# Bias reads at the end of step 4 over two DMA queues, eight products for the first four slots, and the first image's combinations spread over slots 0 to 3

## The chip, the core and the metric

The kernel runs on one core of a Trainium2 chip. A core has five engines that run their own instruction streams: TensorE (PE in the profile, with its weight loads as PEld), VectorE (DVE), ScalarE (ACT), GpSimd (POOL) and SyncE (SP). SP computes nothing here; it issues nearly all DMAs. ACT issues a few DMAs too, between its own operations. An instruction that waits holds up everything behind it on the same engine, and that is true of a DMA-issuing instruction on SP or ACT as well. The metric is the device time of one execution in microseconds (us); lower is better.

## The reference, cut to what matters

The input x has 4 images of 32 by 32 positions with 768 channels. Two layers follow each other. Each one normalizes x over 32 channel groups, runs attention with 12 heads of 64 channels over the 1024 positions of an image, and adds the result to x:

```
x = x + attention0(group_norm(x))
x = x + attention1(group_norm(x))
# attention: q, k, v = x @ W (+ bias in layer 1)
#   scores = scale * q k^T + rel_h[query, key_row] + rel_w[query, key_col]
#   out = softmax(scores) @ v, then @ Wproj + bproj
```

The bias of the scores depends on the query itself: rel_h and rel_w are products of q with a table of 63 relative positions per axis, of which each query uses a different stretch of 32. Everything is float32.

## The kernel before, in words

**Slots and steps.** The 2 layers times 4 images give 8 images in sequence, each with 6 pairs of heads. The 48 pairs are called slots here (`g` in the code, 0 to 47). A slot has 8 steps (`n`), one for each block of 128 queries, so there are 384 steps. All instructions are written out in one fixed order (`tc.manual_schedule`); nothing reorders them later. In the listing, `units` is the list of steps, and the loop over it is the body of the kernel.

**What a step does.** It is a pipeline three steps deep:

- `biases` for the step after next: two POOL additions (L461) spread the two bias axes over 128 x 1024 tiles `sc`, one for each head.
- `scores` for the next step: PE multiplies q and k (L475), DVE combines products and bias and finds the maximum (L484), ACT takes the exponential and its sum (L488).
- `turn` for this step: DVE transposes the finished `sc` into a buffer `tb` (L518). Every second step SP writes `tb` to DRAM as `td` (L521, 1 MB for each head). This covers two steps, a quarter of the slot.
- `divide` for the next step: DVE takes the reciprocal (L495); POOL scales one head (L502), ACT the other (L504).

**Reading back and weighing.** The four quarters of `td` are read back in another order as `pt` (L531, 1 MB for each head), through the lists `behind` and `behind2`: quarter 0 is read at step 3, quarter 1 at step 4, quarter 2 at step 7, and quarter 3 at step 0 of the next slot. A read waits for the write to have landed. At the end of step 6 PE multiplies quarters 0 and 1 with v (L550, `weigh`), and at the end of step 2 of the next slot quarters 2 and 3.

**Work for other slots.** During slot g, PE also runs the projections of slot g+1 (`prepare`), the values of a pair of slots and a share of the output projection of this or the previous image (`put_out`, L629). `shares[n]` says how many pieces of it a step takes after its scores.

**Eight products or seven.** `project_in` has two forms, and `plain(g)` chooses. The plain form multiplies the two halves of q's and k's weights with the two halves of the image: four units of 6 pieces. The other form needs 3.5 units (6, 3, 6 and 6 pieces) but works on sums and differences that have to be made first. Those of the weights are made by `sum_weights` (one ACT copy L330 at the end of step 6 two slots ahead, three POOL operations L333 to L335 at the end of step 7), by a DVE copy (L274) in the middle of unit 0 and a POOL subtraction (L301) after it. Those of the image are made by `sum_input`: it fills spare tiles y and z and changes the image's own tiles in place. In numbers, for an image: 6 ACT copies (L348) and 6 POOL subtractions for y, 6 POOL additions (L351) and 3 ACT copies (L353) for z, then 6 and 6 POOL subtractions in place, all 24 POOL operations on 64 x 512. Before, the plain form is used for the first slot of each image and slot 1:

```
    def plain(g):
        return g % NP == 0 or g == 1
```

For all images but the first, `sum_input` runs in slots 4 and 5 of the image before and in its own slot 0. For the first image it runs in slot 0 (18 POOL operations) and slot 1 (6).

**The bias tables.** `positions(g, i)` multiplies q with the tables on PE (L408), copies the result on ACT (L418), and writes one axis to DRAM as `tdr` from ACT's queue (L420). The other axis is cut out by 32 small ACT copies (L431), which wait in the list `last`, and a step's end takes 8 or 16 of them. `diagonals(g)` reads the first axis back along diagonals into `rel1`: 8 DMAs of 32 KB, 4 for each head (L447). Before, it goes through the list `later`, so that it is issued at the start of step 4 of the slot before. All 8 are on SP, except for slot 0. The POOL addition of step 6 is the first that reads `rel1` for the next slot.

**The order on SP.** In step 4, SP's stream holds: any loads of the next image's x (L117, in the fifth slot of an image), the 8 diagonal reads, a weight load (L131), the first two residual tiles for `put_out` (L608, `fetch`), the read-back of quarter 1; in step 5, two more residual tiles and the write of quarter 2. `fetch` has its place in the step ahead of the read-backs. Its tiles share 4 buffers with the tables' copies.

Of the kernel before, what the change touches and what calls it, by code (L numbers as in the profile page):

```python
# [48 lines left out]
NC = C // P  # L52
# [6 lines left out]
NP = NH // 2  # L59
# [7 lines left out]
def attention_blocks(ctx: ExitStack, tc: tile.TileContext, a: dict, out: bass.AP):  # L67
    nc = tc.nc
# [22 lines left out]
    mid = [dram.tile([C, S], FP, tag=f"mid{b}", name=f"mid{b}") for b in range(B)]  # L91
# [4 lines left out]
    NPAIR = NI * NP  # L96
# [138 lines left out]
    qk_of, v_of, rel_of, t_of = {}, {}, {}, {}  # L235

    def plain(g):
        return g % NP == 0 or g == 1

    def add(to, t, x, bias=None):  # L240

# [94 lines left out]

        return first, second

    def sum_input(im, n):

        xs, ys = x_of[im], y_of[im]

        def each(chunks):
            return [(c, xs[c], xs[NC + c], ys[c], ys[NC + c % 3], TOP if c < 3 else LOW) for c in chunks]

        sub = lambda out, x, y: nc.gpsimd.tensor_tensor(out, x, y, ALU.subtract)  # L346
        for c, a, b, y, z, half in each({-1: (0, 1, 2), 0: (3,), 1: (4,), 2: (5,)}.get(n, ())):
            nc.scalar.copy(y[LOW], b[TOP])  # L348
            sub(y[TOP], b[LOW], y[LOW])
        for c, a, b, y, z, half in each({1: (0,), 2: (1, 2), 3: (3,), 4: (4, 5)}.get(n, ())):  # L350
            nc.gpsimd.tensor_tensor(z[half], y[TOP], a[TOP], ALU.add)  # L351
            if half == TOP:
                nc.scalar.copy(y[LOW], z[TOP])  # L353
        for c, a, b, y, z, half in each({5: (0,), 6: (1, 2), 7: (3, 4, 5)}.get(n, ())):
            sub(b[TOP], b[TOP], a[TOP])
        for c, a, b, y, z, half in each({9: (0, 1, 2), 10: (3, 4, 5)}.get(n, ())):
            sub(y[LOW], (y if half == TOP else z)[LOW], a[LOW])

    def project_values(g, i):

        im, pair = divmod(g, NP)
        xs, w = x_of[im], w_of[g, 2]
        if i == 0:
            for h in range(2):
                v_of[g + h] = vpool.tile([P, NT, P], FP, tag="v", name=f"v_{g + h}")
        t = ps_m.tile([P, 2, 2, 2 * P], FP, tag="m", name=f"pv_{g}_{i}")  # L370
        for k in range(2):
            at = 2 * (i % 2) + k
            for c in range(NC):
                for a in range(2):
                    rows = slice(a * D, (a + 1) * D)
                    nc.tensor.matmul(  # L376
                        t[:, a, k, :],
                        lhsT=xs[i // 2 * NC + c][rows, at * P : (at + 1) * P], rhs=w[rows, c, :],
                        start=(c == 0), stop=(c == NC - 1),
                    )  # L380
                if c % 2 and (k, c) != (1, NC - 1):
                    yield True
        for h in range(2):
            to = v_of[g + h][:, 2 * i : 2 * i + 2, :]
            cols = slice(h * P, (h + 1) * P)
            part = v_of[g + h][:, 2 * i + 4 : 2 * i + 6, :] if i < 2 and g else to
            if i < 2 or g == 0:
                nc.scalar.copy(part, t[:, 0, :, cols])
            else:
                nc.vector.tensor_tensor(to, t[:, 0, :, cols], to, ALU.add)  # L390
            nc.vector.tensor_tensor(to, t[:, 1, :, cols], part, ALU.add)
        if i == 3 and g + 2 < NPAIR:
            later.append(lambda: load_w(g + 2, 2))
        yield True

    def positions(g, i):
# [7 lines left out]
        for j in range(4):  # L404
            for h in range(2):
                rows = slice(h * D, (h + 1) * D)
                at = 4 * i + j
# [24 lines left out]

        last.extend([lambda: rows_axis((0, 1)), lambda: rows_axis((2, 3))])
        if i == 1:
            later.append(lambda: diagonals(g))

    def diagonals(g):
        td = t_of[g]
        for h in range(2):
            for y in range(4):  # L440


                src = bass.AP(
                    td.tensor, td.offset + HW * y * P + h * D + HW - 1,
                    [[P - 1, HW], [P * P, NT], [1, HW]],
                )
                (nc.scalar if h and not g else nc.sync).dma_start(  # L447
                    out=rel_of[g][2][32 * y : 32 * y + 32, h, :, :], in_=src
                )

# [123 lines left out]
    place = {part: at for at, part in enumerate(parts)}  # L574
# [80 lines left out]

    early, mid, later, last, behind, behind2 = [], [], [], [], [], []

    def run(todo):  # L660
        while todo:
            todo.pop(0)()

    def prepare(g):

        todo = [
            (project_in(g, unit), NC // 2 if unit == 1 and not plain(g) else NC)
            for unit in range(4) if g < NPAIR
        ]
        if g % 2:  # L670
            return todo + [(project_values(g - 1, i), NC) for i in (2, 3)]
        return todo + [(project_values(g, i), NC) for i in (0, 1) if g < NPAIR]
# [5 lines left out]
    def take(groups, n):  # L678

        while groups and n > 0:  # L680
            group, count = groups[0]
            if next(group, None) is None:
                groups.pop(0)
            else:
                groups[0] = (group, count - 1)
                n -= 1
        while groups and groups[0][1] == 0:
            for _ in groups.pop(0)[0]:
                pass

    with tc.manual_schedule(engines=ENGINES):
# [13 lines left out]
        take(todo, NC)  # L705
        mid.pop(0)()
        run(last)
        later.pop()()
        take(todo, 2 * NC)
        run(early)  # L710
        run(later)
# [7 lines left out]
        for at, (g, n) in enumerate(units):  # L719
            im, pair = divmod(g, NP)  # L720
# [25 lines left out]
            run(early)  # L746
            early, later = later, early

            upto = 4 * (pair % 3) + 3
            if n in (2, 4, 5) and (im, pair) >= (0, 3):  # L750
                upto -= 2 if n == 4 else 0
                (fetch_weights if n == 2 else fetch)(place[((im, 0) if pair >= 3 else (im - 1, 1)) + divmod(upto, 2)])

            ask = [divmod(g + 3, NP)] if n == 1 else []
            if im == 0 and pair < 3:
                ask = [(0, 2 * pair + n // 4)] if n in (1, 4) else []
# [9 lines left out]
                scores(*units[at + 1])  # L766
            run(behind)
            behind, behind2 = behind2, behind
            if pair == 3 and n in stages and not end:
                stages[n]()  # L770
            share = shares[n]
# [7 lines left out]
            if pair == 4 and not end:  # L779
                for c in {2: (0, 1, 2), 4: (3,), 6: (4, 5, 6), 7: range(7, NX)}.get(n, ()):  # L780
# [1 line left out]
                        take(todo, 3)  # L782
                        share -= 3
                    apply(c % NC, c // NC)
            if g + 2 < NPAIR and not plain(g + 2) and n in (6, 7):
                if n == 6:
                    combine = sum_weights(g + 2)
                combine[n - 6]()
            take(todo, share)
            for k in range(min(len(last), 2 if n == 3 else 1)):  # L790
                last.pop(0)()
            if pair == NP - 2 and n == 7 and not end:
                sum_input(im + 1, -1)
            elif pair == NP - 1 and not end:
                sum_input(im + 1, n)
            elif g == 1 or g and pair == 0:
                sum_input(im, n + NT)
            elif g == 0:
                for k in (-1, 0) if n == 0 else (n,):
                    sum_input(0, k)  # L800
            if n == 6:
                weigh(g, (0, 1))
            elif n == 2 and g:
# [63 lines left out]
```

## Time and profile before

| What | Value |
|---|---|
| Median of 3 runs | 3508.94 us (3507.96 to 3512.74) |
| The profiled execution's own time | 3509.05 us |
| Its span, first to last instruction | 3507.3 us |
| Mean granted clock of TensorE | 0.996 |
| Busy: PE, DVE, POOL, ACT | 3404.6, 2640.3, 2489.6, 1992.0 us |
| DMA: moved, mean rate | 1051.56 MB, 300 GB/s |
| First scores of slot 0 on PE | 56.83 us from the start |

The profile page gives busy times by engine, and lists groups of instructions by line with their mean duration and the idle time ahead of them. The trace can also be asked for waits (who waited for whom), for the timeline of an engine, for the chain of work that ended last, and for busy times in given stretches. DMA-issuing instructions are shown under SPq or ACTq with the time that the issue took, not the transfer. A slot takes about 70 us, a step 6 to 16 us.

### The profile page before, as it was taken

The page shows a single profiled execution, that of the slowest core. Times are in us where ns is not written, and L with a number is a line of the kernel's source. Part 1 is how long each engine was busy: PE and PEld are TensorE (multiplying, and loading weights), DVE is VectorE, ACT ScalarE, POOL GpSimd, SP SyncE. Part 2 cuts the span into 40 slices and gives each one's busy share as a digit, 9 for nine tenths or more (in the row PEclk, how much of TensorE's full clock was granted, in tenths as well). Part 3 has the DMA queues.
Part 4 walks back from the last instruction along what each step waited for, and adds up shares of the span by engine and source line. Part 5 has one row for each costly group of instructions (what it writes and reads, how often), then busy time and mean ns, then how long its engine had stood idle before and what let it go on. Part 6 is the DMA issues. An engine that isn't in the chain of part 4 may idle for free.

```text
span 3507.3 us, 56203 instructions
## 1 busy us (share of the span) xinstructions
PE 3404.6 (97%) x20652; PEld 1906.9 (54%) x20652; DVE 2640.3 (75%) x4011; ACT 1992.0 (57%) x3958; POOL 2489.6 (71%) x1510
## 2 busy tenths in 40 slices
PE   6899999999999999999999999999999999999999
PEld 4455555555555555555555555555555555555554
DVE  4687868778688786787777877777876778777776
ACT  3565556555565556556665566555665566555652
POOL 3876687766866769767686766876678766786663
PEclk9999999999999999999999999999999999999999
DMA  3678988898889887888888898888988889888888
GB/s 115 252 274 321 330 288 307 310 323 327 290 302 328 318 317 270 318 320 320 296 288 316 303 324 289 299 312 302 319 305 300 297 304 327 298 303 299 305 292 289
DMA packets 531221, 1051.56 MB, mean 300 GB/s; under 512 B 143872, under 2 KB 206848, under 8 KB 481792
## 3 DMA queue, kind: packets, MB, share of 16 engines
q1 hardware_dynamic: 476448, 1020.53, 81.0%
q10 hardware_dynamic: 54496, 27.43, 2.6%
q8 instruction: 163, 2.67, 0.3%
q14 instruction: 114, 0.93, 0.1%
HBM read 572.73 MB, written 475.10 MB: 299 GB/s over the span
## 4 chain that ended last, share of the span: by engine, by line
PE 66%; ACT 12%; DMA 8%; DVE 6%; POOL 3%; issue 3%; SPq 1%; ACTq 0%; DVEq 0%; POOLq 0%
PE pj L268 17%; PE av L550 14%; PE s L475 13%; PE o L629 13%; PE pv L376 7%; ACT sc L488 6%; DMA pt<-td 5%; ACT rel L431 3%; ACT sc L504 2%; PE tp L408 2%; DMA td<-tb 2%; DVE x L228 1%; DVE sc L484 1%; DVE tb L518 1%; POOL x L346 1%
## 5 line engine op out<-in xcount | busy, mean ns | idle before, releaser
L461 POOL TENSOR_TENSOR sc<-rel,rel 128x1024 f32<-128x1024 f32 x768 | 1553.3, 2086 | 110.3 <-DVE tb L518 67.6
L488 ACT ACTIVATE sc<-sc,sm 128x1024 f32<-128x1024 f32 x768 | 879.7, 1147 | 927.2 <-DVE sm L484 925.5
L518 DVE STREAM_TRANSPOSE tb<-sc 128x1024 f32<-128x1024 f32 x768 | 944.8, 1234 | 145.4 <-DMA td<-tb 143.8
L484 DVE CUSTOM_DVE_ANT_0 sc<-s,sc 128x1024 f32<-128x1024 f32 x768 | 908.3, 1221 | 149.8 <-PE s L475 141.4
L502 POOL TENSOR_SCALAR sc<-sc,sm 128x1024 f32<-128x1024 f32 x384 | 429.5, 1119 | 804.1 <-DVE sm L495 792.0
L268 PE MATMUL pj<-x,w 64*128 64x512 f32 x4140 | 937.3, 596 | 57.1 <-DVE x L228 26.1
L475 PE MATMUL s<-k,q 64*128 64x512 f32 x3072 | 749.0, 597 | 6.1 <-DVE sm L484 5.9
L550 PE MATMUL av<-pt,v 128*64 128x256 f32 x6144 | 707.5, 383 | 22.8 <-DMA pt<-td 22.8
L268 PEld LDWEIGHTS pj<-x,w 64*128 64x128 f32 x4140 | 421.7, 189 | 545.0 <-issue 451.5
L550 PEld LDWEIGHTS av<-pt,v 128*64 128x64 f32 x6144 | 445.4, 138 | 314.1 <-DMA pt<-td 46.5
L504 ACT ACTIVATE sc<-sc,sm 128x1024 f32<-128x1024 f32 x384 | 441.0, 1148 | 173.6 <-DVE sm L495 173.6
L376 PE MATMUL pv<-wv,x 64*128 64x256 f32 x4608 | 515.1, 376 | 6.8 <-DVE k L243 6.8
L376 PEld LDWEIGHTS pv<-wv,x 64*128 64x128 f32 x4608 | 449.5, 187 | 98.1 <-issue 38.0
L629 PE MATMUL o<-attn,wo 128*128 128x512 f32 x1080 | 478.9, 598 | 4.3 <-DMA wo<-in_wo 1.3
L475 PEld LDWEIGHTS s<-k,q 64*128 64x128 f32 x3072 | 291.5, 187 | 295.9 <-issue 261.8
L431 ACT COPY rel<-t 32x64 f32<-32x64 f32 x1504 | 363.4, 242 | 16.5
L629 PEld LDWEIGHTS o<-attn,wo 128*128 128x128 f32 x1080 | 200.3, 190 | 279.7 <-issue 250.4
L418 ACT COPY t<-tp 128x512 f32<-128x512 f32 x188 | 110.1, 585 | 223.1 <-PE tp L408 169.5
L346 POOL TENSOR_TENSOR x<-x,x 64x512 f32<-64x512 f32 x144 | 183.3, 1292 | 39.6 <-ACT x L348 28.7
L495 DVE RECIPROCAL sm<-sm 128x2 f32<-128x2 f32 x384 | 60.1, 156 | 176.4 <-ACT sc L488 172.4
L243 DVE TENSOR_TENSOR k<-pj,k 128x512 f32<-128x512 f32 x173 | 116.3, 681 | 68.8 <-PE pj L268 44.0
L488 ACT ACTIVATION_READ_ACCUMULATOR sc<-sc,sm 128x1 f32 x768 | 143.2, 186 | 0.0
(54 smaller groups left out, 1575.8 us busy)
## 6 DMA issues: line engine op xcount, KB each, us to landing
td<-tb SPq DMA_DIRECT2D x384, 1024.0 KB, 5.9
pt<-td SPq DMA_DIRECT2D x382, 1024.0 KB, 7.7
w<-in_wqk SPq DMA_DIRECT2D x96, 384.0 KB, 4.8
tdr<-t ACTq DMA_DIRECT2D x94, 256.0 KB, 4.8
x<-in_x SPq DMA_DIRECT2D x84, 256.0 KB, 7.4
part<-res SPq DMA_DIRECT2D x84, 256.0 KB, 5.6
res<-part SPq DMA_DIRECT2D x84, 256.0 KB, 7.8
wv<-in_wv SPq DMA_DIRECT2D x24, 768.0 KB, 13.5
```

Of the source, the lines that this page charges most:

```text
L268: nc.tensor.matmul(t[:, a, :], lhsT=w[a][rows, c, :], rhs=x[c][rows, :], start=(c == 0), stop=(c == len(x) - 1),)
L376: nc.tensor.matmul(t[:, a, k, :], lhsT=xs[i // 2 * NC + c][rows, at * P : (at + 1) * P], rhs=w[rows, c, :], start=(c == 0), stop=(c == NC ...
L431: nc.scalar.copy(rel[of, :, j, :], t[of, j, :, at : at + HW])
L461: nc.gpsimd.tensor_tensor(sc.rearrange("p (a k) (u l) -> p a l (k u)", a=4, l=8), rel0[:, h, :].unsqueeze(1).unsqueeze(2).to_broadcast(shape),
L475: nc.tensor.matmul(ps[h][:, cols], lhsT=q[rows, n * P : (n + 1) * P], rhs=k[rows, cols], start=True, stop=True,)
L484: nc.vector.tensor_tensor_reduce(out=sc, in0=ps[h], in1=sc, scale=-scale, scalar=BIG, op0=ALU.add, op1=ALU.min, accum_out=st[:, 0, h : h + 1],
L488: nc.scalar.activation(sc, sc, AF.Exp, bias=st[:, 0, h : h + 1], scale=-1.0, accum_out=st[:, 1, h : h + 1],)
L502: nc.gpsimd.tensor_scalar(sc, sc, st[:, 2, h : h + 1], 1.0, ALU.mult, ALU.mult)
L504: nc.scalar.activation(sc, sc, AF.Copy, scale=st[:, 2, h : h + 1])
L518: nc.vector.transpose(tb[:, :, j, :], sc_of[g, n, h])
L550: nc.tensor.matmul(av[rows, at * 2 * P : (at + 1) * 2 * P], lhsT=v_of[g][:, k, rows], rhs=pt_of[g, quarter, h][:, :, k, :], start=(k == 0) ...
L629: nc.tensor.matmul(t, lhsT=wo_of[im, o, c], rhs=attn_of[im * NP + c, i], start=(c == c0), stop=(c == c1 - 1),)
```

## The change

There are four parts.

1. **Diagonal reads.** They get a list of their own, `diagonal`, which is run at the end of step 4, after this step's share of PE work and ahead of the small ACT copies. Head 0's four reads stay on SP; head 1's four are issued by ACT in every slot.
2. **Residual and output-weight fetches.** They move behind the read-backs in the step, and the second pair of residual tiles moves from step 5 to step 6.
3. **Eight products for slots 0 to 3.** `plain` holds for slots 2 and 3 as well. `sum_weights` and what belongs to it fall away for these two. The values of slots 2 and 3 are made in the form that slots 0 and 1 have, from the unchanged image (ACT copies in place of four DVE additions).
4. **The first image's combinations.** y is made one chunk a step in steps 2 to 7 of slot 0, z one chunk a step in steps 0 to 5 of slot 1, the first in-place subtractions in steps 5 to 7 of slot 2, the last ones in steps 1 and 2 of slot 3.

```diff
     def plain(g):
-        return g % NP == 0 or g == 1
+        return g % NP == 0 or g < 4
...
-        for c, a, b, y, z, half in each({-1: (0, 1, 2), 0: (3,), 1: (4,), 2: (5,)}.get(n, ())):
+        for c, a, b, y, z, half in each((slow,) if slow is not None and slow < NC else {-1: (0, 1, 2), 0: (3,), 1: (4,), 2: (5,)}.get(n, ())):
             nc.scalar.copy(y[LOW], b[TOP])
             sub(y[TOP], b[LOW], y[LOW])
-        for c, a, b, y, z, half in each({1: (0,), 2: (1, 2), 3: (3,), 4: (4, 5)}.get(n, ())):
+        for c, a, b, y, z, half in each((slow - NC,) if slow is not None and slow >= NC else {1: (0,), 2: (1, 2), 3: (3,), 4: (4, 5)}.get(n, ())):
...
-            part = v_of[g + h][:, 2 * i + 4 : 2 * i + 6, :] if i < 2 and g else to
-            if i < 2 or g == 0:
+            part = v_of[g + h][:, 2 * i + 4 : 2 * i + 6, :] if i < 2 and g > 3 else to
+            if i < 2 or g < 4:
                 nc.scalar.copy(part, t[:, 0, :, cols])
...
         if i == 1:
-            later.append(lambda: diagonals(g))
+            diagonal.append(lambda: diagonals(g))
...
-                (nc.scalar if h and not g else nc.sync).dma_start(
+                (nc.scalar if h else nc.sync).dma_start(
...
-            upto = 4 * (pair % 3) + 3
-            if n in (2, 4, 5) and (im, pair) >= (0, 3):
-                upto -= 2 if n == 4 else 0
-                (fetch_weights if n == 2 else fetch)(place[((im, 0) if pair >= 3 else (im - 1, 1)) + divmod(upto, 2)])
-
...
             run(behind)
             behind, behind2 = behind2, behind
+
+            upto = 4 * (pair % 3) + 3
+            if n in (2, 4, 6) and (im, pair) >= (0, 3):
+                upto -= 2 if n == 4 else 0
+                (fetch_weights if n == 2 else fetch)(place[((im, 0) if pair >= 3 else (im - 1, 1)) + divmod(upto, 2)])
...
             take(todo, share)
+            if n == 4:
+                run(diagonal)
...
-            elif g == 1 or g and pair == 0:
+            elif g == 3 or g and pair == 0:
                 sum_input(im, n + NT)
-            elif g == 0:
-                for k in (-1, 0) if n == 0 else (n,):
-                    sum_input(0, k)
+            elif g == 2 and n > 4:
+                sum_input(0, n)
+            elif g < 2 and 1 < at < 2 + 2 * NC:
+                sum_input(0, None, at - 2)
```

## The prediction

> **What bounds the kernel now.** The page's first two parts come first:
>
> ```profile
> PE 3404.6 (97%) x20652; PEld 1906.9 (54%) x20652; DVE 2640.3 (75%) x4011; ACT 1992.0 (57%) x3958; POOL 2489.6 (71%) x1510
> ...
> PE   6899999999999999999999999999999999999999
> ```
>
> PE looks like the bound everywhere but in the first 175 us. Busy time hides waits inside overlapping matmuls, so I count PE's work from undisturbed runs in the chain of work: L268 takes 7.72 us for 36, L475 1.72 for 8, L376 5.18 for 48, L550 7.06 for 64, L408 1.09 for 16, L629 10.50 for 24. A slot whose successor uses the seven-product form needs 84, 64, 96, 128, 32 and 24 of them: 18.0 + 13.8 + 10.4 + 14.1 + 2.2 + 10.5 = 69.0 us. Busy times by stretch follow, for slots 0 to 3 and slot 14 (slots cut at the first transpose of their step 0):
>
> ```profile
> core 0: us, PE busy (x) PEld busy (x) DVE busy (x) ACT busy (x) POOL busy (x), PEclk, DMA share, GB/s
> 69.10:145.70 76.60, 67.44 (x382) 38.43 (x378) 49.68 (x77) 49.15 (x98) 65.84 (x45) 0.96 0.67 241
> 145.70:219.50 73.80, 64.63 (x406) 36.04 (x406) 54.33 (x78) 40.61 (x82) 60.20 (x37) 0.95 0.76 274
> 219.50:287.80 68.30, 62.83 (x406) 36.66 (x406) 55.57 (x82) 39.34 (x78) 47.78 (x28) 0.98 0.82 292
> 287.80:356.20 68.40, 67.90 (x412) 39.41 (x414) 52.98 (x86) 42.74 (x84) 47.85 (x28) 0.98 0.86 300
> 1078.90:1148.20 69.30, 69.25 (x430) 39.13 (x428) 57.03 (x88) 39.36 (x78) 47.98 (x28) 1.00 0.89 322
> ```
>
> Slot 14 takes 69.3: PE-bound, nothing to gain there. Slots 0 to 2 take 76.6, 73.8 and 68.3 though their PE work without the output projection is 59.3, 58.5 and 58.5. POOL is busiest where they are longest.
>
> Next the waits over the whole span (waiter, releaser, us in total, times, longest):
>
> ```profile
> DVE tb L518 <- DMA td<-tb: 143.8, 43, 6.9
> ...
> PEld av L550 <- DMA pt<-td: 46.5, 46, 2.6
> ...
> PE av L550 <- DMA pt<-td: 22.8, 22, 2.1
> ```
>
> The first stalls DVE, not PE. PE's main wait in the long PE-bound part is for the read-back: 46.5 us. I checked it by the length of each block of 64 L550 matmuls: all blocks at step 2 take 7.06, those at step 6 take 46.4 more in sum. Of this 1.5 is in slots 1 and 2, 2.1 in the last slot, where the order does not change, and 42.9 in slots 4 to 46; 25.0 of that in the seven "fifth slots" of an image (13.8 in slot 4, 13.1 in slot 10). SP's timeline in slot 12 shows why:
>
> ```profile
> 965.95 1.79 SPq L521 DMA_DIRECT2D td<-tb  x2
> 967.84 6.06 SPq L447 DMA_DIRECT2D rel<-tdr  x8
> 974.02 1.61 SPq L131 DMA_DIRECT2D w<-in_wqk  x1
> 975.67 0.91 SPq L608 DMA_DIRECT2D res<-part  x2
> 976.62 0.98 SPq L531 DMA_DIRECT2D pt<-td  x2
> 977.70 1.11 SPq L608 DMA_DIRECT2D res<-part  x2
> 980.15 1.78 SPq L521 DMA_DIRECT2D td<-tb  x2
> ```
>
> The writes of quarter 1 land 3.9 and 5.2 us after their issue (969.9 and 972.6), but the reads go out at 976.6 and 977.1: eight small reads take 6.06 us of SP's time ahead of them. The chain of work runs through just these: L521, eight L447, L131, L608, L531, "977.10 10.33 DMA pt<-td", then PE at 987.47. PE had begun the block at 982.84 and needed the data at 986.4 (half of 7.06 later).
>
> **What the Trainium skill says.** "DMA: Bandwidth & Descriptors", section "Issuing engines are not separate DMA queues": DMAs of all engines share the same 16 DMA engines, and another issuer saves only sequencer time. The 6.06 us above are sequencer time. Section "Queues, rings and completion order": each engine consumes one queue's ring in order and alternates between queues. The trace agrees for SP: the second read waits behind the first (landings 984.7 and 987.4), and the td writes issued at 980.15 land 11.2 us later, behind both. "SBUF — State Buffer", section "Who interferes with whom": a DVE copy in a two-port mode and a GpSimd operation exclude each other. The trace agrees: L274 takes 4.09 us at 283.64 beside two L461 of POOL, against a mean of 0.99.
>
> **Part 1 and 2: SP's order, slots 4 to 46.** The reads of quarter 1 now come right after the weight load, so they can go out when their writes have landed: 4 to 7 us earlier in slot 12. In SP's order of data, the weight tile would land by 974, then two reads of 1 MB at 2.7 to 3.9 us each (the gaps between landings): 977.5 and 980.5, where 987.4 was and 986.4 is needed. The wait is gone. In slot 10 the three x tiles stay ahead (last landing 828.9); weight tile 830.4, reads 833.3 and 836.2 against 841.2 before and 837.0 needed: gone too. But there DVE is late next: its second transpose of step 6 waited 6.2 us for the write of quarter 2 (landing 845.0). That write moves up with the rest to about 841.2, as two residual tiles no longer stand ahead of it; DVE's later work in that slot is dense, so PE's output projection gains about 3.8 of 6.0. I take 4, 3.8 and 3.5 for slots 4, 10 and 28, and all of the other four (2.3 + 2.0 + 2.4 + 1.2): 19. Of the other 17.9 I take 90%: 16. Together **-35**; from 0, if the writes' landing is what binds, to -43 and, with the shorter DVE waits, -50.
>
> What it costs: ACT issues four DMAs more. Before slot 0 these took 0.34 to 0.47 each (ACT, L447), so 1.8 us in each slot between L504 and the eight L431 of step 4. In slot 12, L431 would end at 979.1 rather than 977.1, and the exponential of step 5 (977.85) is late by 1.3. Then the reciprocal and the second transpose are; the next scores' L484 has its products at 982.8 and is late by under 1; PE does not wait for it before the 7 us of L550 are over. Nothing in PE-bound slots; I put 1 us for each of slots 0 to 2: **+3** (0 to +8 with slots 5, 11 and so on, where POOL is 84% busy).
>
> The diagonal reads come later. The first POOL addition needing them was at 981.62 in slot 12. SP's four now land behind read-back and residuals, at about 982.4 by the sum above; ACT's four go out at 975 to 977 and share the engines with 2 MB of read-back: 4 to 8 us (the other DMA on ACT's queue took 4.8), so 979 to 985. POOL may wait some 1 to 3 us. Its two additions (4.0) are first used by L484 at about 993, so 6 to 7 us are free: cost 0. No wait of `tdr` is added on ACT: its write went out at 961.2 and landed 3.9 later. The residual tiles fetched at step 6 go out after 982 behind 2 to 3 MB, so by about 992; the third group of L629 needs them after 998: 0. The weight fetch of step 2 has no read-back to pass: 0.
>
> **Parts 3 and 4: slots 0 to 3.** Of slot 0's 18 operations L346 and L351 (22.5 us) 12 go elsewhere, and the weights' 5.4 us (L333 to L335) fall away; PE's work stays.
>
> ```profile
> ACT x L353 <- POOL x L351: 9.4, 3, 6.0
> ```
>
> This wait (ACT's waits, 78 to 126 us) holds ACT's exponentials: steps 2 and 3 took 12.0 and 12.3 us, and without it about 6.5 and 7. Step 7 took 11.5 since DVE's L274 waited for POOL's L335; now about 6.5. The fuller PE (step 4 has 12 pieces, as before) pays some of it back: I set slot 0 to 62.7 (steps 8.1, 8.1, 6.5, 8, 10, 7.5, 8, 6.5; PE's work 59.3). Slot 1 gets 12 matmuls more, 2.6 us, but loses L274, L301 and the 14.4 us of step 1 (PE waited for L301). Slot 5, whose successor is plain, has steps 6.1, 6.9, 10.2, 11.7, 9.4, 6.8, 9.5; with 6.3 for a step 7 without output projection: 66.9. Slot 2 likewise, but its step 7 keeps the combination for slot 4 as slot 0 had it (11.5): 72.1. Slot 3 inherits what slot 1 had: POOL full at the turn, step 1 of 14.4 rather than 9.5, 10.2 rather than 9.9; 73.6. Sum 275.3 against 287.1: **-12**. The three ACT copies (0.57) more and L330 (0.83) less in the plain form are in slot 5's steps. Bounds: slots 1 and 2 may overlap worse (-3), or all four come near PE's 250.5 plus turns (-19).
>
> **Sum.** 3509.05 - 35 + 3 - 12 = 3465.05; the extra early waits of slots 1 and 2 (1.5) go too: 3463.5. The profiled execution stands 0.1 above the median, so I forecast 3464 for the median.
>
> **Rivals.** *Early part only.* The landing is set by the DMA engines (share 0.89, 322 GB/s in slot 14), and the wait just moves to other transfers: 10 of 35 gained, 3509 - 10 + 3 - 12 = 3490. For it: 143.8 us of DVE waits on writes. Against: in slot 12 nothing was queued between 973 and 976 but 32 KB reads. *Late part only.* Slots 2 and 3 pay what slots 0 and 1 gain: 3509 - 35 + 3 = 3477. For it: the same POOL work is only moved, and PE gets 5.2 us more. Against: slot 1's PE idled 15 us. *Slower: late diagonals.* If ACT's 128-byte rows get through only after the read-back and SP's four queue behind more than I count, POOL waits over 7 us at step 6 and L484 waits for POOL. From there each us costs up to 1 in 43 slots; 1.1 us over the slack eats the whole gain, 2 us over give 3509 - 47 + 86 = 3548. Against: 6 to 7 us of slack. *Even.* Half of each gain and some lateness: 3509.
>
> **How the numbers follow.** The least I call a change is 0.2%, 7 us, about what a measurement here can tell. Forecast 0.58 (own range 3450 to 3482), early only 0.14, late only 0.14, even 0.07, slower 0.07. Faster 0.86, same 0.07, slower 0.07. The range takes in the two partial rivals and the sum's better bounds (3509 - 43 - 19 = 3447): 3447 to 3497.
>
> **What would show it.** The wait of L550 for `pt` falls from 46.5 to under 10 us; L531 of quarter 1 follows L131 in SP's timeline at step 4; waits of L518 for `td` fall below 120. L461's wait for `rel` stays small; if it is tens of us beyond the start's 35.9, the slower rival is at work. Slots 0 and 1 fall to about 63 and 67, slots 2 and 3 rise to about 72 and 74. The prediction fails if reads issued earlier land no earlier, or if ACT's four issues take much over 0.5 us each.

## The result, and the profile after

The changed kernel takes 3636.27 us (median of 4 runs, 3624.93 to 3641.82), beside 3510.84 us (3507.96 to 3514.44) for the kernel before on the same chip. The ratio is 1.035, with an interval of 1.032 to 1.038: slower by 3.5%, where 3464 us were forecast. The profiled execution took 3633.11 us. One line was added near the top of the file, so lines of the kernel before appear with one more in what follows: L448 is the diagonal read, L432 the small copy into `rel`, L489 the exponential, L532 the read-back.

The page of the changed kernel, busy time by engine and the chain of work that ended last:

```profile
PE 3471.6 (96%) x20676; PEld 1911.6 (53%) x20676; DVE 2632.5 (72%) x3997; ACT 2000.4 (55%) x3966; POOL 2472.0 (68%) x1502
...
PE 52%; DMA 16%; ACT 16%; DVE 8%; issue 4%; POOL 4%; SPq 0%; ACTq 0%; DVEq 0%; POOLq 0%
```

By the first line nothing has happened: PE is still at 96%, and DVE, ACT and POOL do the work they did. Busy time cannot tell what went wrong here. The waits over the whole span of the changed kernel can (waiter, releaser, us in total, times, longest):

```profile
DVE sm L496 <- ACT sc L489: 392.8, 257, 7.9
...
ACT rel L432 <- DMA rel<-tdr: 202.3, 36, 7.7
...
POOL sc L462 <- DMA rel<-tdr: 65.2, 9, 35.4
...
DVE tb L519 <- DMA td<-tb: 10.8, 7, 2.2
...
PEld av L551 <- DMA pt<-td: 1.2, 1, 1.2
```

The last two lines are what the change was about, and both have gone as forecast or further: PE waited 46.5 us for the read-back and waits 1.2, DVE waited 143.8 us for the writes and waits 10.8. The second line is new. `L432` copies from SBUF to SBUF; it needs nothing from a DMA of `rel<-tdr`. It merely stands behind one on ACT. And DVE's wait for ACT's exponential rose to 392.8 from what it was in the kernel before:

```profile
DVE sm L495 <- ACT sc L488: 172.4, 269, 6.3
```

ACT's timeline in slot 12 of the changed kernel (start, length, what, and in brackets the idle time ahead) shows where:

```profile
988.54 1.15 ACT L505 ACTIVATE sc<-sc,sm 128x1024 f32<-128x1024 f32 x1 [0.23 <-DVE sm L496]
988.60 7.85 ACTq L448 DMA_DIRECT2D rel<-tdr  x4
996.49 2.02 ACT L432 COPY rel<-t 32x64 f32<-32x64 f32 x8 [6.80 <-DMA rel<-tdr]
998.54 1.15 ACT L489 ACTIVATE sc<-sc,sm 128x1024 f32<-128x1024 f32 x1
```

In the kernel before, ACT's same three operations followed each other with 0.78 us between the second and the third:

```profile
974.02 1.15 ACT L504 ACTIVATE sc<-sc,sm 128x1024 f32<-128x1024 f32 x1 [0.23 <-DVE sm L495]
975.07 2.01 ACT L431 COPY rel<-t 32x64 f32<-32x64 f32 x8
977.85 1.15 ACT L488 ACTIVATE sc<-sc,sm 128x1024 f32<-128x1024 f32 x1 [0.78 <-DVE sm L484]
```

The four issues, priced at 0.34 to 0.47 us each, stretch over 7.85 us. The exponential of the next step is behind them: it starts 12.3 us after the start of step 4, where it started 6.2 us after it before. DVE and PE of the changed kernel in the same place:

```profile
993.40 1.24 DVE L519 STREAM_TRANSPOSE tb<-sc 128x1024 f32<-128x1024 f32 x1
1000.94 0.17 DVE L496 RECIPROCAL sm<-sm 128x2 f32<-128x2 f32 x1 [6.30 <-ACT sc L489]
1001.03 1.22 DVE L519 STREAM_TRANSPOSE tb<-sc 128x1024 f32<-128x1024 f32 x1
```

```profile
997.37 2.81 PE L551 MATMUL av<-pt,v 128*64 128x256 f32 x24
1003.07 4.54 PE L551 MATMUL av<-pt,v 128*64 128x256 f32 x40 [2.90 <-DVE v L392]
```

DVE's reciprocal waits for the exponential, its transpose and its additions of v (L391, L392) stand behind the reciprocal, and PE's block L551 waits for those. Step 5 of slot 12 takes 12.6 us, where it took 6.5 before. SP's timeline there:

```profile
980.48 1.79 SPq L522 DMA_DIRECT2D td<-tb  x2
982.37 0.96 SPq L132 DMA_DIRECT2D w<-in_wqk  x1
984.46 3.75 SPq L532 DMA_DIRECT2D pt<-td  x2
988.26 1.19 SPq L609 DMA_DIRECT2D res<-part  x2
989.50 8.54 SPq L448 DMA_DIRECT2D rel<-tdr  x4
```

The read-back follows the weight load, as the prediction asked. But SP's four diagonal reads, too, take 8.54 us, of which the four issues themselves are 1.5.

**What holds a DMA.** In the trace every DMA of SP and ACT carries the number of the semaphore that counts its completion. There are eight of them in all (100 to 103 and 105 to 108), used in turn over the DMAs of both engines in one common order. This order keeps that of the code within each engine, but not between the two: in slot 12 ACT's first read has semaphore 103, and SP's second residual tile, which the code loads earlier, has 105. The table is worked out from the trace of slot 12 of the changed kernel; the last three columns are the DMA that used the same semaphore before, which is the one eight places ahead, when it landed, and how long after that this one was issued.

| Issued | By | DMA | Semaphore | Eight places ahead | Landed | Issued after |
|---|---|---|---|---|---|---|
| 984.46 | SP | pt | 100 | w | 967.55 | 16.9 |
| 987.84 | SP | pt | 101 | tdr | 968.30 | 19.5 |
| 988.60 | ACT | rel, first | 103 | pt, quarter 0 | 978.76 | 9.8 |
| 988.96 | ACT | rel, second | 106 | td | 984.39 | 4.6 |
| 989.79 | ACT | rel, third | 108 | w | 988.76 | 1.0 |
| 992.98 | SP | rel | 100 | pt of 984.46 | 992.97 | 0.02 |
| 996.14 | ACT | rel, fourth | 101 | pt of 987.84 | 996.12 | 0.02 |
| 997.24 | SP | rel | 102 | res | 997.23 | 0.02 |

The instruction list of the built program says the same of ACT's four reads in this slot. It numbers the eight semaphores 0 to 7, so that 3 to 5 are 103, 105 and 106, 7 is 108, and 1 is 101:

```
L448 DMACopy rel1_13_6792<-tdr_13_6791 32x8x32 [waits DMAHW4_49,DMAHW3_49]
L448 DMACopy rel1_13_6792<-tdr_13_6791 32x8x32 [waits DMAHW5_49]
L448 DMACopy rel1_13_6792<-tdr_13_6791 32x8x32 [waits DMAHW7_49]
L448 DMACopy rel1_13_6792<-tdr_13_6791 32x8x32 [waits DMAHW1_49]
```

Only the first waits for data (`tdr`, semaphore 105). Every one waits for the DMA eight places ahead. Over all 1992 DMAs of SP and ACT in this list the eight semaphores follow each other without a break. In the trace of the kernel before, 1984 DMAs have one eight places ahead with a known landing; not one was issued before that landing, and the closest came 0.016 us after it. In the changed kernel, 107 of ACT's 188 reads in slots 0 to 46 were issued within 0.03 us of it, and in 44 of the 107 that landing was one of the read-back, in another 44 one of a residual tile. From the end of ACT's operation ahead of the four to the end of the fourth issue it is 6.05 us in the median slot, 241.9 us in sum over these 47. So ACT, which computes, stood still until a transfer of SP's, most often a large one, had landed. The Trainium skill gives a possible motive ("DMA: Bandwidth & Descriptors", section "Why a DMA increments its semaphore by 16 and not by 1"): with two DMAs in flight on one semaphore, a wait for the first can pass too early. No run here shows that; they show only the spacing.

This reading had to be tested: the late place of the reads, the small rows of 128 bytes or ACT's queue itself could slow them as well. In the expectations below, W (later R) is this reading, P puts the loss down to the late place, and Q to ACT's queue and its small rows, later to any four DMAs on ACT.

### The profile page after: what moved, and what is told of

Its sections match the earlier page's. It is cut to its first block, busy times and chain, and to the rows that moved or that the text cites. A ratio compares the mean times of both kernels' runs of the same rounds, so it can differ in the third digit from the quotient of the medians.

```text
span 3631.2 us, 56256 instructions
## 1 busy us (share of the span) xinstructions
PE 3471.6 (96%) x20676; PEld 1911.6 (53%) x20676; DVE 2632.5 (72%) x3997; ACT 2000.4 (55%) x3966; POOL 2472.0 (68%) x1502
## 4 chain that ended last, share of the span: by engine, by line
PE 52%; DMA 16%; ACT 16%; DVE 8%; issue 4%; POOL 4%; SPq 0%; ACTq 0%; DVEq 0%; POOLq 0%
PE pj L269 13%; PE o L630 12%; PE s L476 11%; PE av L551 11%; ACT sc L489 8%; DMA td<-tb 6%; DMA pt<-td 5%; ACT rel L432 4%; DVE tb L519 2%; DMA rel<-tdr 2%; PE pv L377 2%; PE tp L409 2%; ACT sc L505 2%; DVE x L229 2%; DVE sc L485 1%
## 5 line engine op out<-in xcount | busy, mean ns | idle before, releaser
L489 ACT ACTIVATE sc<-sc,sm 128x1024 f32<-128x1024 f32 x768 | 879.5, 1146 | 769.7 <-DVE sm L485 767.3
L269 PE MATMUL pj<-x,w 64*128 64x512 f32 x4164 | 950.8, 597 | 53.8 <-DVE x L229 26.4
L519 DVE STREAM_TRANSPOSE tb<-sc 128x1024 f32<-128x1024 f32 x768 | 944.6, 1233 | 12.3 <-DMA td<-tb 10.8
L476 PE MATMUL s<-k,q 64*128 64x512 f32 x3072 | 792.1, 609 | 40.7 <-DVE sm L485 40.4
L551 PE MATMUL av<-pt,v 128*64 128x256 f32 x6144 | 701.8, 386 | 43.4 <-DVE v L392 42.6
L551 PEld LDWEIGHTS av<-pt,v 128*64 128x64 f32 x6144 | 437.4, 139 | 337.0 <-issue 56.7
L630 PE MATMUL o<-attn,wo 128*128 128x512 f32 x1080 | 502.3, 620 | 11.1 <-DVE attn L560 5.1
L432 ACT COPY rel<-t 32x64 f32<-32x64 f32 x1504 | 363.7, 242 | 252.9 <-DMA rel<-tdr 194.9
L476 PEld LDWEIGHTS s<-k,q 64*128 64x128 f32 x3072 | 305.5, 189 | 349.5 <-issue 257.9
L630 PEld LDWEIGHTS o<-attn,wo 128*128 128x128 f32 x1080 | 208.2, 198 | 310.8 <-issue 254.2
L496 DVE RECIPROCAL sm<-sm 128x2 f32<-128x2 f32 x384 | 60.0, 156 | 398.8 <-ACT sc L489 392.8
L489 ACT ACTIVATION_READ_ACCUMULATOR sc<-sc,sm 128x1 f32 x768 | 143.3, 187 | 0.0
```

The costliest lines, as they stand in the source:

```text
L269: nc.tensor.matmul(t[:, a, :], lhsT=w[a][rows, c, :], rhs=x[c][rows, :], start=(c == 0), stop=(c == len(x) - 1),)
L432: nc.scalar.copy(rel[of, :, j, :], t[of, j, :, at : at + HW])
L476: nc.tensor.matmul(ps[h][:, cols], lhsT=q[rows, n * P : (n + 1) * P], rhs=k[rows, cols], start=True, stop=True,)
L489: nc.scalar.activation(sc, sc, AF.Exp, bias=st[:, 0, h : h + 1], scale=-1.0, accum_out=st[:, 1, h : h + 1],)
L519: nc.vector.transpose(tb[:, :, j, :], sc_of[g, n, h])
L551: nc.tensor.matmul(av[rows, at * 2 * P : (at + 1) * 2 * P], lhsT=v_of[g][:, k, rows], rhs=pt_of[g, quarter, h][:, :, k, :], start=(k == 0) ...
```

## The experiments

Each ratio is to the kernel before on the same chip, where that took 3510.4 to 3512.1 us in the median.

**All eight reads on SP.** The changed kernel with one expression altered, so that ACT issues none after slot 0:

```diff
-                (nc.scalar if h else nc.sync).dma_start(
+                (nc.scalar if h and not g else nc.sync).dma_start(
```

> The changed kernel with all eight diagonal reads on SP, still at the end of step 4. Theory W (rotation: a DMA waits until the DMA eight places before it has landed, so ACT's four reads are held by the read-back of quarter 1 and the residuals, and ACT with them): L432's wait for rel goes from 202 us to under 10, step 5 from 12 to 14 us back to 7 or 8, time 3460 to 3490, as SP can be held without ACT. Theory P (place: the reads at the end of step 4 come too late, whoever issues them): step 5 stays over 11 us, time over 3600. Theory Q (ACT's own queue is slow for 128-byte rows): as W.

Measured: 3462.24 us (3459.33 to 3465.73), ratio 0.986 [0.985, 0.988] to the kernel before. The waits of this kernel:

```profile
POOL sc L462 <- DMA rel<-tdr: 112.1, 32, 34.5
...
DVE tb L519 <- DMA td<-tb: 37.3, 28, 3.9
...
PEld av L551 <- DMA pt<-td: 2.3, 1, 2.3
```

The whole loss of 174 us hangs on that one expression. The wait of L432 has gone, step 5 of slot 12 is back at 6.5 us, and the time is the one that was forecast for the full change. P is out, since the reads stand at the same place as in the changed kernel. W and Q both expected this. SP is still held (in slot 12 four of its eight reads went out 0.016 to 0.017 us after the landing eight places ahead), but SP computes nothing, and no loss follows. POOL waits longer than in the changed kernel (112.1 us, 34.5 of them at the start) and it costs PE nothing that can be seen: slots 12 to 15 take 70.7, 69.2, 69.2 and 68.5.

By the trace, of the 170.3 us between the two spans (3631.2 and 3460.9) 87.8 are longer PE time (3471.6 against 3383.8) and the other 82.5 are idle PE, with a mean granted clock of 0.981 against 0.997. Busy times by stretch, slot 3 and slot 14 (columns as in the prediction: PE, PEld, DVE, ACT, POOL, granted clock, DMA share, GB/s), first of the changed kernel:

```profile
273.30:353.00 79.70, 74.93 (x414) 40.25 (x416) 53.01 (x88) 42.91 (x84) 60.34 (x37) 0.91 0.73 255
1097.70:1172.50 74.80, 70.83 (x428) 39.16 (x426) 57.04 (x89) 39.45 (x78) 47.85 (x28) 0.98 0.85 298
```

and of the kernel with all eight on SP:

```profile
266.40:339.70 73.30, 69.28 (x412) 38.59 (x414) 53.03 (x86) 42.74 (x84) 60.33 (x37) 0.95 0.83 284
1052.20:1121.40 69.20, 69.20 (x430) 38.67 (x428) 57.19 (x89) 39.36 (x78) 47.80 (x28) 1.00 0.89 319
```

In slot 14, 5.6 us are lost: about 4.0 of them are idle PE, and 1.6 are PE time at a lower granted clock (the first figure after POOL's).

**Head 1's reads on ACT at the old place.** The changed kernel with the diagonal reads back at the start of step 4, head 1's four still on ACT:

```diff
-            diagonal.append(lambda: diagonals(g))
+            later.append(lambda: diagonals(g))
```

> The changed kernel with the diagonal reads back at the start of step 4, head 1's four still on ACT. W: there the eighth-last DMAs are the writes of quarter 1, landed within 1 to 2 us of ACT's turn, so ACT is held 1 to 2 us a slot: 3470 to 3520. P: as fast as with SP alone there, 3470 to 3500. Q: four reads on ACT's queue still hold ACT, step 5 or 4 stays 4 us longer: over 3580.

Measured: 3482.31 us (3481.97 to 3486.33), ratio 0.992 [0.991, 0.994]. ACT's four issues now take 2.37 us in the median slot rather than 5.06 (first issue to last), 117.7 in sum over slots 0 to 46. The same 128-byte reads on the same queue, with fewer fresh landings eight places ahead (15 of the 188 were issued within 0.03 us of one, not 107), cost a ninth of the loss (3482.3 against 3462.7 with all on SP at that place, below). That they are slow in themselves, as Q had it, falls.

**At the end of step 5.** The changed kernel with its reads one step later, when quarter 1's read-back is past:

```diff
-            if n == 4:
+            if n == 5:
                 run(diagonal)
```

> The changed kernel with the eight reads (four on ACT) at the end of step 5, a step later. W: by then the read-back has nearly landed, ACT is held under 2 us, POOL waits some us for rel at step 6, most of it in its slack: 3470 to 3540. P: a step later is worse than the changed kernel: over 3640. Q: as slow as the changed kernel, about 3630.

Measured: 3580.88 us (3577.66 to 3582.76), ratio 1.020 [1.018, 1.021]. Missed, by 41 us at the least. ACT was held as before (4.87 us in the median slot), now by the landings of the write of quarter 2 and of earlier diagonal reads; and the reads were late for POOL, as the waits show:

```profile
POOL sc L462 <- DMA rel<-tdr: 367.0, 54, 34.5
ACT sc L489 <- DMA rel<-tdr: 158.4, 33, 7.3
```

I had reckoned with the read-back alone. Here ACT's hold and the late place both act, so this run separates little.

**The early part alone.** The kernel before with parts 3 and 4 only:

```diff
-        return g % NP == 0 or g == 1
+        return g % NP == 0 or g < 4
...
-            elif g == 1 or g and pair == 0:
+            elif g == 3 or g and pair == 0:
...
+            elif g == 2 and n > 4:
+                sum_input(0, n)
+            elif g < 2 and 1 < at < 2 + 2 * NC:
+                sum_input(0, None, at - 2)
```

> The kernel before with only the parts for slots 0 to 3 (eight products, spread combinations). Forecast by the sum of the prediction: 12 us less than before, 3490 to 3502; slots 0 and 1 about 63 and 67, slots 2 and 3 about 72 and 74. If the moved POOL work costs as much as it gives: within 5 of before. All three theories on ACT expect the same here: no loss in later slots.

Measured: 3493.44 us (3485.0 to 3496.29), ratio 0.995 [0.993, 0.997], 17.9 us less than before. Slots 0 to 3 take 62.2, 65.3, 70.0 and 74.5. The later slots keep what they had:

```profile
DVE tb L519 <- DMA td<-tb: 139.0, 42, 6.9
...
PEld av L551 <- DMA pt<-td: 44.0, 39, 3.5
```

**Four small DMAs on ACT that nobody needs.** If the rotation holds ACT, any DMA at this place must do it. To the kernel with all eight reads on SP, four writes of 3 KB were added in slots 0 to 46, of data long there, to DRAM that nobody reads:

```diff
             if n == 4:
                 run(diagonal)
+                for k in range(4 if g + 1 < NPAIR else 0):
+                    tiny = dram2.tile([P, NC], FP, tag=f"tiny{k}", name=f"tiny_{g}_{k}")
+                    nc.scalar.dma_start(out=tiny, in_=bo[0])
```

> This is the changed kernel with all eight diagonal reads on SP (3462 us), plus work that nothing needs: in slots 0 to 46 ACT issues four DMAs of 3 KB (SBUF to DRAM) at the end of step 4, where the changed kernel issued head 1's four reads. The data are ready, and nobody waits for the result. Rotation theory R (every DMA of the program waits until the one eight places ahead of it in program order has landed, so an engine that issues one between SP's bulk transfers stands still until a bulk transfer lands): ACT's four issues take 3 to 6 us a slot again, L432 of step 4 is late, and the time is 3540 to 3640 us. Rival Q (ACT was held because reads of tdr on its queue wait for their data, or because 128-byte rows are slow there): these DMAs wait for no data and have long rows, ACT's four issues take under 2 us, and the time is 3455 to 3480.

Measured: 3636.92 us (3632.62 to 3643.53), ratio 1.036 [1.034, 1.038]. 12 KB a slot that nothing waits for cost 175 us beside the kernel with all eight on SP (3462.24). The size of the hold was forecast too evenly. ACT's timeline in slot 13 of this kernel:

```profile
1061.74 0.37 ACT L389 COPY v<-pv 128x256 f32<-128x256 f32 x1 [0.49 <-DVE v L392]
1068.08 2.32 ACTq L797 DMA_DIRECT2D tiny<-bo  x4
1070.44 2.02 ACT L432 COPY rel<-t 32x64 f32<-32x64 f32 x8 [8.33 <-DMA tiny<-bo]
```

and in slot 14:

```profile
1136.65 1.15 ACT L505 ACTIVATE sc<-sc,sm 128x1024 f32<-128x1024 f32 x1 [0.23 <-DVE sm L496]
1136.66 1.82 ACTq L797 DMA_DIRECT2D tiny<-bo  x4
1138.52 2.02 ACT L432 COPY rel<-t 32x64 f32<-32x64 f32 x8 [0.72 <-issue]
```

The same four writes, in the same step: ACT stands idle 8.3 us in slot 13 (most of it ahead of the first issue, where an issue's own row does not show it) and 0.7 in slot 14. From slot 7 on, this goes with the number of the slot: the 20 odd ones are 124 us longer than with all on SP, the 20 even ones 23. In the odd slots the four stand behind SP's eight diagonal reads in the common order, and the DMA eight places ahead of the first is one of those; it was issued 0.022 us after that had landed. In most even slots they stand ahead of the diagonal reads, and what is eight places ahead (pt of quarter 0, tdr, td, w) had landed 8.3, 8.0, 1.5 and 1.0 us earlier in slot 14.

**The same four, another place in the order.** One move: ahead of the step's share of PE work rather than behind it. On ACT this passes two copies L389 in slots 13 and 15 and nothing in slot 12 or 14.

```diff
+            for k in range(4 if n == 4 and g + 1 < NPAIR else 0):
+                tiny = dram2.tile([P, NC], FP, tag=f"tiny{k}", name=f"tiny_{g}_{k}")
+                nc.scalar.dma_start(out=tiny, in_=bo[0])
             take(todo, share)
             if n == 4:
                 run(diagonal)
-                for k in range(4 if g + 1 < NPAIR else 0):
-                    tiny = dram2.tile([P, NC], FP, tag=f"tiny{k}", name=f"tiny_{g}_{k}")
-                    nc.scalar.dma_start(out=tiny, in_=bo[0])
```

> As tiny_on_act (3637 us): all eight diagonal reads on SP, and four 3 KB DMAs on ACT in step 4 of slots 0 to 46 that nothing needs. One edit: ACT issues them ahead of step 4's share of PE work instead of behind it. In ACT's own stream this moves them, in the odd slots, ahead of two small copies (L389); in the even slots they stay between the same two instructions. What changes is their place in the program's order of DMAs: in the odd slots (13, 15) they stood behind SP's diagonal reads, so that the DMA eight places ahead was one of those reads, and ACT stood 7 to 9 us; now they stand before the second residual tile, as in the even slots, and the one eight places ahead landed long before. Rotation theory R: the hold in the odd slots falls from 7.2 to 9.4 us to 2 or 3, step 5 of odd slots from 15 to 7 to 8 us, and the time to 3470 to 3520. Rival Q (four DMAs on ACT at this time of a slot cost what they cost, whatever their place in that order): odd slots stay at 75 to 78 us, 3600 to 3640.

Measured: 3584.3 us (3581.02 to 3584.7), ratio 1.021 [1.019, 1.022]: 53 us better than at the other place, but 64 above the range that I gave. Slot 13 did what was expected; ACT's timeline there:

```profile
1058.13 1.15 ACT L505 ACTIVATE sc<-sc,sm 128x1024 f32<-128x1024 f32 x1 [0.23 <-DVE sm L496]
1058.14 2.04 ACTq L794 DMA_DIRECT2D tiny<-bo  x4
1060.22 0.37 ACT L389 COPY v<-pv 128x256 f32<-128x256 f32 x1 [0.94 <-PE s L476]
```

ACT's idle time fell from 8.3 to 0.9 us and the slot from 76.8 to 69.2 us, so it is the place in the order and not the four DMAs. Slots 19, 25, 31, 37 and 43 went likewise, with 0.8 to 2.1 us. But in slot 15:

```profile
1197.92 6.28 ACTq L794 DMA_DIRECT2D tiny<-bo  x2
1204.24 0.37 ACT L389 COPY v<-pv 128x256 f32<-128x256 f32 x1 [5.46 <-DMA pt<-td]
```

Here another DMA had slipped in, and the fourth write stood eight places behind the fresh read-back: it was issued 0.02 us after that had landed. Slots 9, 15, 21, 27, 33 and 39 stay at some 75 us. Slots 11, 17, 23, 29, 35 and 41 became slower, 78.6 to 80.7 us from 74.5 to 75.5: there the third and the fourth write now stand eight places behind a fresh read-back and a residual tile, and were issued 0.02 us after these had landed. I had expected all odd slots to shift alike and had worked out only slots 13 and 15, the latter wrongly. The theory holds; my count of places did not.

**The two moves on SP, each alone.** First the kernel before with the diagonal reads (all on SP) at the end of step 4 and nothing else:

```diff
-            later.append(lambda: diagonals(g))
+            diagonal.append(lambda: diagonals(g))
...
             take(todo, share)
+            if n == 4:
+                run(diagonal)
```

> The kernel before with one edit: the eight diagonal reads, all on SP, move from the start to the end of step 4. The residual fetches, slots 0 to 3 and ACT stay as before. If the place of the diagonal reads is what made the read-back late, nearly all of the 31 us that the early part is worth (all_on_sp 3462 against early_only 3493) comes from here: 3480 to 3492. If the fetches ahead of the read-back hold it as much, half: 3492 to 3500. If the two only work together, 3500 to 3512.

Measured: 3489.86 us (3488.56 to 3491.96), ratio 0.994 [0.992, 0.996]: 22 us less. Its waits:

```profile
DVE tb L518 <- DMA td<-tb: 115.5, 40, 6.0
POOL sc L461 <- DMA rel<-tdr: 113.1, 34, 34.4
...
PEld av L550 <- DMA pt<-td: 1.9, 2, 1.1
```

Then the kernel before with the fetches moved and nothing else:

```diff
-            if n in (2, 4, 5) and (im, pair) >= (0, 3):
+            if n in (2, 4, 6) and (im, pair) >= (0, 3):
```

(these lines, with the calls under them, now behind `run(behind)`).

> The kernel before with one edit: the residual and output-weight fetches move behind the read-backs, and the second pair from step 5 to step 6. The eight diagonal reads stay ahead of the read-back. If the diagonal reads alone make it late: 3502 to 3512. If the two residual tiles ahead of the write of quarter 2 matter (the fifth slots' DVE wait): 3490 to 3502.

Measured: 3480.36 us (3478.53 to 3485.97), ratio 0.991 [0.989, 0.993]: 32 us less, far more than I gave it. Its waits:

```profile
DVE tb L518 <- DMA td<-tb: 73.5, 32, 5.5
POOL sc L461 <- DMA rel<-tdr: 36.2, 2, 34.8
...
PEld av L550 <- DMA pt<-td: 10.6, 8, 2.5
```

Either move alone ends most of PE's wait for the read-back, since each takes something off SP ahead of it. In slot 12 the second read landed 15.7 us after the start of step 4 in the kernel before, 11.4 with the diagonal move, 13.4 with the fetch move, and it is needed at 14.7 (986.4 by the prediction, less 971.7). The fetch move also takes two residual tiles from ahead of the write of quarter 2 and leaves POOL's reads early; DVE's wait for writes falls to 73.5, not 115.5.

**The changed kernel without part 1.** Diagonal reads at the start of step 4 on SP, all else as changed:

```diff
-            diagonal.append(lambda: diagonals(g))
+            (later if g else diagonal).append(lambda: diagonals(g))
...
-                (nc.scalar if h else nc.sync).dma_start(
+                (nc.scalar if h and not g else nc.sync).dma_start(
```

> The changed kernel without its part 1: the eight diagonal reads are at the start of step 4, all on SP, as in the kernel before; the fetches behind the read-backs and the early part (slots 0 to 3) are kept. If the two gains measured alone add up (fetch move 32, early part 18): 3462, between 3456 and 3468, and then moving the diagonal reads is worth nothing beside the fetch move. If the move of the diagonal reads adds its own share (22 alone), this is slower than all_on_sp by up to 20: 3470 to 3482.

Measured: 3462.71 us (3459.59 to 3467.37), ratio 0.986 [0.985, 0.988]. That is the kernel with all eight reads moved on SP (3462.24) again: beside the fetch move, moving the diagonal reads is worth nothing. Against old_place_act, which differs from this kernel only in that ACT issues head 1's four, it is 19.6 us faster. So even at the better place the four on ACT cost 0.4 us a slot.

**The reads in two halves.** All on SP; head 0's four at the start of step 4, head 1's at its end:

```diff
-            diagonal.append(lambda: diagonals(g))
+            if g == 0:
+                diagonal.append(lambda: diagonals(g))
+            else:
+                later.append(lambda: diagonals(g, (0,)))
+                diagonal.append(lambda: diagonals(g, (1,)))
```

> All diagonal reads on SP; head 0's four go out at the start of step 4, as in the kernel before, head 1's four stay at the end of step 4, behind the read-back of quarter 1; the rest as in the changed kernel. SP stands idle for some us at the start of step 4 until the write of quarter 1 has landed; four reads take about 3 us of it. If the gap is long enough, the read-back is as early as with all eight behind it, and POOL's wait for rel (112 us, all eight behind) falls: 3445 to 3462. If the gap is too short, or the read-back itself now waits eight places back for a landing, L551's wait comes back in part: 3462 to 3485. I take 3458.

Measured: 3456.77 us (3453.23 to 3457.93), ratio 0.984 [0.982, 0.986]: 55 us below the kernel before and the lowest median of all. In slot 12, SP issues head 0's reads (940.67 to 944.75) while the write of quarter 1 is landing (942.7 and 945.5), and the read-back goes out at 945.29 and 945.77. From the start of step 4 that is 0.8 and 1.3 us, where with all eight behind it was 1.8 us ahead of the start and 1.7 us after it; the second read lands at 10.5 rather than 9.3, and is needed at 14.7. So head 0's reads do hold up the first half of the read-back here, within the slack. The interval overlaps those of the two kernels at 3462, so the runs do not show that it beats these.

## Why the prediction was wrong

**The step that failed is "What it costs: ACT issues four DMAs more".** It priced ACT's issues at 0.34 to 0.47 us each, 1.8 us a slot, from ACT's reads ahead of slot 0, where no bulk transfer stood eight places ahead. Measured, they hold ACT for 6.05 us in the median slot; the exponential of step 5 in slot 12, forecast late by 1.3 us, is late by 6.2. And it costed that at "Nothing in PE-bound slots; ... +3", with the 7 us of L551 as cover. The cover is real but small: with the tiny writes 0.7 to 2.4 us of hold in the even slots 8 to 44 pass nearly unseen (18 us over 19 slots), 4.7 to 5.8 us in slots 11, 17 and so on cost 2 to 3, and the 7.2 to 9.4 us of the other odd slots from 7 on cost 7.8 in the mean. The term was +3 and measures +174 (3636.3 less 3462.2).

**A clue was in the profile before.** "No wait of `tdr` is added on ACT" looked at data alone. The waits of SP's queue in the kernel before have this line:

```profile
SPq L447 <- DMA x<-in_x: 5.3, 8, 1.4
```

A read of `tdr` needs nothing from x, so it must have waited for something else than its data. In slot 12, which the prediction shows, there was nothing to see: each of SP's eight reads went out 0.87 us or more after the landing eight places ahead. The line comes from the slots that load x: in slot 10 the eighth read went out 0.016 us after an x tile had landed. The condition "if ACT's four issues take much over 0.5 us each" was the right thing to watch, but it was written as a way to fail and given no price. The Trainium skill's sentence that another issuer saves only sequencer time ("DMA: Bandwidth & Descriptors", section "Issuing engines are not separate DMA queues") speaks of the transfers and of the time to issue them. It says nothing of the waits that come along with an issue; here these stopped the engine, and SP's waits were moved onto one with work to do.

**Parts 1 and 2 on SP: right in mechanism, near in size.** Forecast -35; 31.2 with ACT left out (3493.44 less 3462.24). The seven fifth slots gave 14.0 us where 19 were forecast, the other slots from 5 to 46 15.2 where 16 were. The wait of L551 fell below 10 us and L532 follows the weight load, as listed. But the credit was misplaced: in slots other than the fifth the prediction put it down to the diagonal reads, and the fetch move alone gives all of it (3462.71 with the diagonal reads left where they were).

**The late diagonal reads: right.** POOL's wait for `rel` rose by some 29 us in the changed kernel and by 76 with all on SP, the latter at no cost that shows (3462.24, and 3462.71 with the reads at the old place), so the rival "Slower: late diagonals" is not what happened. Its sign, a wait tens of us beyond the start's 35.9, did come and was a false one. The forecast's slower case had the right sign and the wrong engine: it was ACT that waited, for landings that it needed nothing from.

**Parts 3 and 4: right, a little low.** Forecast -12, measured -17.9 in time and -15.2 over slots 0 to 3. Forecast for these slots 62.7, 66.9, 72.1 and 73.6; alone 62.2, 65.3, 70.0 and 74.5. "Late part only" falls with this, and "early part only" with the 31 us of the other parts.

**The sum.** Without the failed term it is 3509.05 - 35 - 12 - 1.5 = 3460.6, and the kernel that leaves out just that edit takes 3462.24. That is in part luck: two of the errors inside it, 5 us too many for parts 1 and 2 (36.5 against 31.2) and 6 too few for parts 3 and 4, happen to cancel.

## What to carry to other kernels

Before DMAs are moved to a computing engine, find what each one waits for besides its data: here the DMA eight places ahead over both issuing engines, so that a 3 KB write among 1 MB transfers can stop its issuer until one of these, or a small DMA that went out behind it, has landed. Such an edit is priced by the landings that stand that many places ahead, not by the issue's length in a quiet place, and small DMAs among bulk transfers belong on an engine that has nothing else to do. Where two edits take work off the same queue ahead of the same transfer, test each alone, since the first may take all the gain.

## What was not expected of the hardware

- A held issue need not look long. In slot 13 with the tiny writes ACT stood 8.3 us and the row of the four shows 2.32. The Trainium skill says that a DMA's reported start is the moment when its semaphores are satisfied ("Perfetto Trace Analysis", section "DMA Instruction — HWDGE (DVE, Sync)"), and the trace agrees: of the 8.3 us, some 6 lie ahead of the first row. The idle time of the next operation on the engine is what tells.
- Idle stretches on PE went with a lower granted clock: 0.981 over the changed kernel and 0.997 with all reads on SP, and in slot 3, 0.91 against 0.95. PE's booked time rose by 88 us for the same work. The tie is loose: with the reads at the end of step 5, PE was idle for 136.9 us of the span at a clock of 0.992, with the tiny writes at their second place for 145.7 us at 0.981. What of the 88 us is clock, and what is waiting inside pipelined matmuls, these runs do not separate.
